# Rounds of five attention units with expert tiles in a new order, in a fused transformer block on one core

## The chip, the core and the metric

The kernel runs on one core of a Trainium2 chip. The metric is the device time of one execution in microseconds. TensorE is called PE, VectorE DVE, ScalarE ACT, GpSimd POOL, and SyncE, which here issues most DMA transfers, SP.

## The reference

The reference is a pre-norm transformer block over 2048 tokens of width 512, all in float32. After a layer norm, two parts run on the same normalised tokens, and both results are added to the input:

```python
xn = _layernorm(x)
x  = x + attention(xn) + moe(xn)

# attention: 16 heads, each with two score maps (q1,k1), (q2,k2) of width 16
s      = einsum('bthd,bshd->bhts', q, k) * scale          # q, k with interleaved rotary
a      = softmax(where(causal, s, NEG))
attn_i = concatenate([a_i @ v1, a_i @ v2])                # i = 1, 2; 32 columns per head
f      = rfft(attn1, axis=tokens) - lambda * rfft(attn2, axis=tokens)
attn   = irfft(f * gaussian_filter, axis=tokens)
attn   = attn * rsqrt(mean(attn*attn over a head's 32) + eps) * rms_weight * (1 - LAMBDA_INIT)
out    = attn @ Wout

# moe: 8 experts of inner width 352, top 2 of a softmax gate with renormalised weights
y      = sum_k topk_w[k] * (silu(x @ w1[e_k]) * (x @ w3[e_k])) @ w2[e_k]
shared = (silu(x @ sw1) * (x @ sw3)) @ sw2                # inner width 704
```

## The kernel before

**Stages.** The first 366 us hold the layer norm, the projections, the gate with its top-2, the rotary step and the first tokens of the shared expert. The stage that the change is mostly about is `middle(general=False)`: attention scores and values, with the experts' work laid between them. `ending()` then runs the token filter as products with fixed matrices (`product`, L1141), the head norm (`Pair`), the output projection (`projected`, L1270) and the last additions (`finished`, `last`).

**Who decides the order.** In `middle` and in `ending` the schedule is written by hand: PE, DVE, ACT, POOL (in `middle` SP too) execute their instructions in the order in which the Python code calls them, each waiting for what it needs. There is no reordering. Buffers come from pools that rotate: a new tile of a tag takes the oldest buffer and waits until its last reader is done.

**Attention units.** Work is cut by `turns`: eight groups `g` of two heads, and in each the query chunks `qc` = 3, 2, 1, 0 of 512 tokens. A turn consists of units (`Chunk.units`); a plain unit is one head and one block of 128 keys against 512 queries. Near the diagonal, units have fewer columns and are masked. There are 544 units (`stream`). For a unit, `scores` multiplies keys with queries for both score maps (PE, `ps_s`, L822), takes the exponential on ACT (L835, `pt`) and, where masked, zeroes what lies above the diagonal on POOL (`affine_select`, L840). `values` multiplies both heads' `pt` with the values (PE, `ps_o`, L862, 4 products for each block of keys, each of which is two instructions in the profile). `added` sums the exponentials over keys on DVE (L876, L879). When a turn ends, `sums` (PE, `ps_sum`, L888), `finish` (PE transposes into `ps_ot` and `ps_st`, then DVE: reciprocal `rcp` L903, `o_n` L908) and `put` (POOL, L917) follow. When a group's four turns have ended, `folded` does the group's butterflies over the tokens in steps on POOL, the last group's on DVE (L947 to L970).

**A round.** The loop at L1029 takes four units: `burst` of two (their scores), the `values` of the oldest turn that are due, a turn's `sums`, `burst` of the other two, the remaining `values`, then `put`, `finish`, the adds (those of masked units at the end), and steps of the experts' work (`work`), as many as keep pace with the share of `stream` that is done. Then come up to two steps of `folded`. At the first unit of a turn, `burst` also issues on SP the loads of the next turn's queries (`load_queries`: 8 transfers `qS` of 64 KB) and of the next group's keys (`load_keys`: 4 transfers `kS` of 128 KB, which read each row for two places of the tile by a leading broadcast of 2).

**Experts.** `experts()` is a generator that yields between pieces of work. It runs the shared expert for tokens 512 to 1919, then 34 tiles (`NR`) of 128 routed tokens. The first 28 (`NP`) hold tokens of one expert, the last 6 of two experts, 64 rows each. The rows are gathered by `rows_of` (POOL). A tile goes through a transpose (`ps_x`, L165), two up products (`xh` and `xg`, L180), an activation and a multiplication (`xtanh` on ACT and DVE), a transpose (`ps_u`, L206, copied as `uT` by DVE), the down product (`xy`, L216) and a store (`y_sb`, scaled on ACT, to `ys`). Weights lie in two buffers, `w_sb[0]` and `w_sb[1]`, each with an up part `wu` (1408 KB) and a down part `wd` (768 KB). Tiles of one expert take the buffers in turn; a tile of two experts uses both at once. `fetch_up` for the next but one half is issued on SP behind the `xg` products, and `fetch_down` behind `xy`. In the remaining 128 tokens, `kept`, the shared expert runs in `ending` (`several`, PE `wh` L246).

**PSUM.** There are 8 banks: scores have two buffers of two banks (`sps`), `ps_o` one, and everything else in `middle` shares the three banks of `fps` by `bank()`, in a fixed rotation: `wh`, `wy`, `ps_x`, `xh`, `xg`, `ps_u`, `xy`, `ps_sum`, `ps_ot`, `ps_st`.

**The end stage.** In `ending`, pools `t1`, `tp` serve all tiles in SBUF. `still(k)` issues the loads and gathers for later output tiles (`fetched`: query rows on SP, accumulating transfers on POOL). `across` transposes a scaled tile for `projected`; `Pair` starts with `y` and its square, and `means` and `scales` make the norm.

Of the kernel before, what the change touches and what calls it, by code (L numbers as in the profile page):

```python
# [19 lines left out]
P = 128  # L20
T = 2048
E = 512
# [24 lines left out]

NP = (T * TOP // HALF - NX) // 2
WUP = NE * 2 * FI
WCOL = WUP + NF * E  # L50
# [17 lines left out]
def block_kernel(  # L68
# [527 lines left out]
    def middle(general):  # L596


        with ExitStack() as pools:
# [29 lines left out]
            def experts():  # L629
# [7 lines left out]
                for t0 in range(EARLY, NT - 1, TQ):  # L637
                    t1 = min(t0 + TQ, NT - 1)
                    last = t1 == NT - 1
                    cols = slice(t0 * P, t1 * P)  # L640
                    for n, us in enumerate(chunks(xnT[:, :, cols], u_last)):
                        if last and n == 0:
                            who_sb = mp.tile([P, E], F32, tag="x", name="who_sb")
                            who_sb = who_sb[:NR].rearrange("n (k p o) -> n k p o", k=TOP, o=2)
                            for k in range(TOP):
                                nc.sync.dma_start(who_sb[:, k], who[k][: NR * P, :].rearrange("(n p) o -> n p o", p=P))
                        elif last and n == 2:
                            nc.vector.tensor_add(who_sb[:, 0], who_sb[:, 0], who_sb[:, 1])
                        elif last and n == 3:
                            ps = bank([P, 2, NR], "ps_w")  # L650
                            for i in range(2):
                                nc.tensor.transpose(ps[:, i, :], who_sb[:, 0, :, i], ident[:NR, :NR])
                            nc.vector.tensor_copy(tok, ps[:, 0, :])
                            nc.vector.tensor_copy(wcol, ps[:, 1, :])
                        elif last and n == 5:


                            xr = [rows_of(0), rows_of(1)]
                            es = [routed(0)]
                            fetch_up(es[0], 0, nc.sync)  # L660
                        yield 3.45 * (t1 - t0) / TQ
                    if last:
                        es.append(routed(2))
                        fetch_up(es[1], 1, nc.sync)
                    for t in range(t0, t1):
                        y = result(us, t - t0, range(NF))
                        yield 2.6
                        stored(result(us, t - t0, range(NF, SCH), y), ysh[t], 0.5)
                        yield 2.6
# [7 lines left out]

                sets = [[j] if j < NP else [2 * j - NP, 2 * j - NP + 1] for j in range(NR)]
                halves = [2 * j + i for j in range(NR) for i in range(len(sets[j]))]

# [3 lines left out]
                def tile_down(j, uT):  # L684
                    return places(j, 1), uT, ys[j * P : (j + 1) * P, :], wcol[:, j : j + 1]

                for j in range(NR):
# [5 lines left out]
                    if j + 2 < NR:  # L693
                        xr.append(rows_of(j + 2))
                    for n in sets[j]:
# [61 lines left out]
            def greatest(g, qc):  # L757
# [29 lines left out]
                return shift  # L787

            class Chunk:

# [19 lines left out]

                def scores(self, unit):
# [4 lines left out]
                    ps = sps.tile([P, 2, QC], F32, tag="sc", name="ps_s")  # L816
                    for h, kb, off, col, w in unit:
                        for s in range(2):
                            r = slice(64 * s, 64 * s + 64)
                            k = keys[2 * g + h, kb // TQ][r, kb % TQ * P : (kb % TQ + 1) * P]  # L820
                            to = ps[:, s, col : col + w]
                            nc.tensor.matmul(  # L822
# [11 lines left out]
                    used = slice(min(c for *_, c, _ in unit), max(c + w for *_, c, w in unit))  # L834
                    nc.scalar.activation(pt[:, :, used], ps[:, :, used], AF.Exp, scale=SCALE)  # L835
                    for _, kb, _, col, _ in unit:
                        if kb >= qc * TQ and not general:

                            part = pt[:, :, col : col + P]
                            nc.gpsimd.affine_select(  # L840
                                out=part, in_=part, pattern=[[0, 2], [1, P]], compare_op=ALU.is_ge, fill=0.0,
                                base=0, channel_multiplier=-1,
                            )
# [140 lines left out]
            for c in range(NQC):  # L984
                load_keys(0, c)
                if c == 0:
                    load_queries(0, NQC - 1)
            worked, begun, summed, held = 0.0, -1, 0, []
            todo, closing, closed, shared, ready, folding = [], [], [], [], [], None

            def burst(units):
                nonlocal begun
                found = []
                for n, chunk, unit in units:
                    if n > begun:
                        begun = n
                        if n + 1 < len(turns):
                            load_queries(*turns[n + 1])

                        if chunk.g + 1 < NG:  # L1000
                            load_keys(chunk.g + 1, (chunk.qc + 1) % NQC)
                    found += chunk.scores(unit)
                return found
# [12 lines left out]

            def masked(entry):
                _, c, unit = entry
                return any(kb >= c.qc * TQ for _, kb, *_ in unit)

            def added(entries):
# [6 lines left out]

            for i in range(0, len(stream), 4):  # L1029
                units = stream[i : i + 4]  # L1030
                found = burst(units[:2])
                n, ended = values()
# [3 lines left out]
                if n < 2 and not closing:  # L1036

                    work()
                found += burst(units[2:])
                while todo:  # L1040
# [10 lines left out]
                added(before)  # L1051
                added(u for u in units[:2] if not masked(u))
                later = [u for u in units[2:] if not masked(u)]
                while True:
                    work()
                    added(later[:1])
                    later = later[1:]
                    if worked / (work_all - left) >= (i + 4) / len(stream):
                        break
                added(later)  # L1060
                added(u for u in units if masked(u))
                if any(map(masked, units)) or not shared:
                    steps = 0
                else:
                    steps = 1 if any(map(masked, stream[i + 4 : i + 8])) else 2
                for _ in range(steps):
                    if folding is None and ready:
                        folding = folded(ready.pop(0), nc.gpsimd)
                    if folding is not None and next(folding, 0) == 0:
                        folding = None  # L1070
# [20 lines left out]
    def ending():  # L1091

        with tc.tile_pool(name="tail1", bufs=1) as t1, tc.tile_pool(name="tail", bufs=2) as tp, tc.tile_pool(
            name="tail_ps", bufs=4, space=PSUM
        ) as fps, tc.tile_pool(name="conv_ps", bufs=2, space=PSUM) as zps, tc.manual_schedule(
            engines={mybir.EngineType.PE, mybir.EngineType.DVE, mybir.EngineType.Activation, mybir.EngineType.Pool}
# [3 lines left out]
            nc.scalar.dma_start(conv[:, 11 * P :], conv_t[:, 11 * P :])  # L1102
            _, _, _, _, (_, _, stored), _ = expert(tp, fps)
            hidden, gated, times, _, result = shared_expert(tp, fps, 2)
            fetch_down(wex[NX + 1 : NX + 2], 1, nc.scalar)
# [46 lines left out]
            def copied(z):  # L1152
                diff = tp.tile([P, 2, E], F32, tag="diff", name="diff")
                nc.scalar.copy(diff, z)
# [27 lines left out]
            product(zr[:, 1, :], [(1, vd[:, 1, :])])  # L1182
            first = tp.tile([P, E], F32, tag="first", name="first", bufs=1)
            nc.scalar.copy(first, zr[:, 1, :])
# [127 lines left out]
            for n in range(NT // 2):  # L1312
# [157 lines left out]
```

## Time and profile before

| quantity | value |
|---|---|
| time, median of 3 runs | 1360.07 us (1357.98 to 1361.46) |
| profiled execution, own time | 1360.14 us |
| its span | 1358.3 us, 1.84 us less than its own time |
| granted TensorE clock, mean | 0.994 |
| PE busy in the span | 1312.6 us (97%) |
| DVE, ACT, POOL busy | 1005.4, 688.4, 626.3 us |
| 366 to 1186 us (units beside experts) | PE 808.43 of 820, DVE 667.37, ACT 534.43, POOL 492.18 |
| 1186 to 1242 us (last units and expert tiles) | PE 47.61 of 56 |
| 1242 to 1358 us (end stage) | PE 102.80 of 116, DVE 78.48, POOL 69.63 |

The durations are of one profiled execution, whose time lies 0.07 us from the median. In the profile's rows, "L822" is the line of the program that issued the instruction, `out<-in` names what it writes and reads, and a row that ends in "x4" joins four neighbouring instructions of one kind.

### The profile page before, as it was taken

The page shows a single profiled execution, that of the slowest core. Times are in us where ns is not written, and L with a number is a line of the kernel's source. Part 1 is how long each engine was busy: PE and PEld are TensorE (multiplying, and loading weights), DVE is VectorE, ACT ScalarE, POOL GpSimd, SP SyncE. Part 2 cuts the span into 40 slices and gives each one's busy share as a digit, 9 for nine tenths or more (in the row PEclk, how much of TensorE's full clock was granted, in tenths as well). Part 3 has the DMA queues.
Part 4 walks back from the last instruction along what each step waited for, and adds up shares of the span by engine and source line. Part 5 has one row for each costly group of instructions (what it writes and reads, how often), then busy time and mean ns, then how long its engine had stood idle before and what let it go on. Part 6 is the DMA issues. An engine that isn't in the chain of part 4 may idle for free.

```text
span 1358.3 us, 20810 instructions
## 1 busy us (share of the span) xinstructions
PE 1312.6 (97%) x7554; PEld 600.3 (44%) x7554; DVE 1005.4 (74%) x1344; ACT 688.4 (51%) x847; POOL 626.3 (46%) x671
## 2 busy tenths in 40 slices
PE   7999999999999999999999999899999999987998
PEld 3444444334443444445444444344544444443544
DVE  7049883287668778868889986778898788764785
ACT  2311110265656566676666666566676666640221
POOL 0002330012221323235968984778589469421764
PEclk9999999999999999999999999999999999998999
DMA  9406673200211122235665656555565666777997
GB/s 375 171 16 171 201 196 97 89 15 32 75 43 31 40 75 82 74 123 170 190 194 143 226 176 180 181 173 174 185 194 178 210 189 230 262 294 293 175 219 169
DMA packets 75578, 214.29 MB, mean 158 GB/s; under 512 B 12244, under 2 KB 12696, under 8 KB 69576
## 3 DMA queue, kind: packets, MB, share of 16 engines
q1 hardware_dynamic: 62744, 185.68, 41.7%
q0 software_dynamic: 11056, 22.78, 8.6%
q10 hardware_dynamic: 1664, 4.38, 0.9%
q8 instruction: 63, 1.03, 0.3%
q14 instruction: 51, 0.42, 0.1%
HBM read 169.69 MB, written 43.10 MB: 157 GB/s over the span
## 4 chain that ended last, share of the span: by engine, by line
PE 65%; DVE 6%; POOL 5%; DMA 3%; issue 1%; ACT 1%; SPq 0%; DVEq 0%; ACTq 0%; POOLq 0%
PE ps_o L862 16%; PE ps_s L822 12%; PE wh L246 8%; PE xy L216 6%; PE xg L180 5%; PE xh L180 5%; PE wy L284 4%; PE ps_sum L888 2%; DMA wu<-in_wex_dram 2%; POOL pt L840 1%; PE po L1270 1%; DMA wd<-in_wex_dram 1%; DVE sum L879 1%; PE ps_ot L900 1%; PE ps_x L165 1%
## 5 line engine op out<-in xcount | busy, mean ns | idle before, releaser
L879 DVE TENSOR_TENSOR sum<-sum,pt 128x1024 f32<-128x1024 f32 (+3 forms) x576 | 621.4, 1128 | 36.3 <-ACT pt L835 21.6
L835 ACT ACTIVATE pt<-ps_s 128x1024 f32<-128x1024 f32 x544 | 527.3, 1023 | 184.3 <-PE ps_s L822 131.0
L840 POOL TENSOR_SCALAR_AFFINE_SELECT pt<-pt 128x256 f32<-128x256 f32 x256 | 171.0, 693 | 358.7 <-ACT pt L835 357.5
L862 PE MATMUL ps_o<-pt,vd 128*32 128x512 f32 (+3 forms) x2560 | 268.0, 534 | 4.1 <-POOL pt L840 4.1
L822 PE MATMUL ps_s<-qS,kS 64*128 64x512 f32 (+3 forms) x1280 | 203.8, 406 | 2.0 <-DVEq L1335 1.6
L822 PEld LDWEIGHTS ps_s<-qS,kS 64*128 64x128 f32 x1280 | 97.1, 185 | 177.0 <-issue 95.9
L246 PE MATMUL wh<-xnT,wu 128*128 128x512 f32 (+1 forms) x352 | 150.4, 574 | 0.0
L862 PEld LDWEIGHTS ps_o<-pt,vd 128*32 128x32 f32 x2560 | 66.9, 109 | 125.8 <-issue 103.5
L545 PE MATMUL ps_x<-xnT,wqk_sb 128*128 128x512 f32 x256 | 110.5, 593 | 0.0
L498 POOL DMA_INDIRECT who<-pairs,slot x32 | 33.1, 1034 | 165.9 <-DVE pairs L495 104.9
L216 PE MATMUL xy<-wd,uT 128*128 128x512 f32 (+3 forms) x240 | 97.1, 606 | 7.7 <-DVE rcp L903 6.3
L246 PEld LDWEIGHTS wh<-xnT,wu 128*128 128x128 f32 x352 | 64.1, 190 | 72.7 <-issue 56.5
L180 PE MATMUL xh<-wu,xT 128*128 128x352 f32 (+1 forms) x320 | 90.5, 473 | 4.2 <-DMA wu<-in_wex_dram 3.3
L917 POOL TENSOR_TENSOR vd<-o_n 128x128 f32<-128x128 f32 x60 | 62.2, 1057 | 65.6 <-DVE o_n L908 65.5
L180 PE MATMUL xg<-wu,xT 128*128 128x352 f32 (+1 forms) x320 | 88.6, 468 | 0.0
L545 PEld LDWEIGHTS ps_x<-xnT,wqk_sb 128*128 128x128 f32 x256 | 48.4, 190 | 60.6 <-issue 60.6
L284 PE MATMUL wy<-wd,ws 128*128 128x512 f32 x160 | 74.8, 603 | 0.0
L257 DVE SCALAR_TENSOR_TENSOR ws<-ws,wh 128x512 f32<-128x512 f32 (+4 forms) x26 | 16.7, 644 | 73.6 <-ACT ws L256 73.6
L1125 POOL DMA_INDIRECT res<-ys,slot x32 | 54.9, 1715 | 25.3 <-DMA res<-ysh 13.5
L562 ACT CAST hi<-turned 128x1024 fp32r<-128x1024 f32 x16 | 16.7, 1045 | 93.9 <-DVE turned L560 70.9
L180 PEld LDWEIGHTS xh<-wu,xT 128*128 128x128 f32 (+1 forms) x320 | 48.0, 176 | 31.7 <-issue 6.5
L180 PEld LDWEIGHTS xg<-wu,xT 128*128 128x128 f32 (+1 forms) x320 | 46.6, 174 | 34.4 <-issue 14.8
(254 smaller groups left out, 1416.8 us busy)
## 6 DMA issues: line engine op xcount, KB each, us to landing
wu<-in_wex_dram SPq DMA_DIRECT2D x44, 1408.0 KB
wd<-in_wex_dram SPq DMA_DIRECT2D x43, 768.0 KB
kS<-parts_k SPq DMA_DIRECT2D x128, 128.0 KB
qS<-parts_q SPq DMA_DIRECT2D x256, 64.0 KB
ys<-y_sb SPq DMA_DIRECT2D x34, 256.0 KB
parts_q<-hi SPq DMA_DIRECT2D x32, 256.0 KB
parts_k<-hi SPq DMA_DIRECT2D x16, 256.0 KB
parts_k<-turned SPq DMA_DIRECT2D x16, 256.0 KB
```

Source lines behind the costliest of these rows:

```text
L180: nc.tensor.matmul(dst[r, :], xT[:, c, r], w[:, o : o + FI], start=(c == 0), stop=(c == NE - 1), skip_group_check=True,)
L216: nc.tensor.matmul(y[r, :], uT[:m, ic, r], w[:m, ic * E : (ic + 1) * E], start=(ic == 0), stop=(ic == NF - 1), skip_group_check=True,)
L246: nc.tensor.matmul(dst, w_sb[o // WUP][0][:, o % WUP : o % WUP + P], x[:, c, :], start=(c == 0), stop=(c == NE - 1))
L284: nc.tensor.matmul(y, us[i][:, t * P : (t + 1) * P], w_sb[i // NF][1][:, i % NF * E : (i % NF + 1) * E], start=(i == 0), stop=(i == SCH - 1),)
L545: nc.tensor.matmul(ps[:, i, :], wqk_sb[st, qk][:, i, c, :], xnT[:, c, cols], start=(c == 0), stop=(c == NE - 1),)
L822: nc.tensor.matmul(to, k, queries[2 * g + h, qc][r, off : off + w], start=True, stop=not general)
L835: nc.scalar.activation(pt[:, :, used], ps[:, :, used], AF.Exp, scale=SCALE)
L840: nc.gpsimd.affine_select(out=part, in_=part, pattern=[[0, 2], [1, P]], compare_op=ALU.is_ge, fill=0.0, base=0, channel_multiplier=-1,)
L862: nc.tensor.matmul(self.o[r : r + 32, off:], vd[:, kb, v0 : v0 + 32], pt[:, s, :], start=first, stop=self.ended, skip_group_check=True,)
L879: nc.vector.tensor_add(to, to, pt)
L917: eng.tensor_add(vd[:, self.qc * TQ : (self.qc + 1) * TQ, v0 : v0 + 32], self.o_n[:, :, h, 0, :], self.o_n[:, :, h, 1, :],)
L1125: nc.gpsimd.indirect_dma_start(out=came[k], out_offset=None, in_=ys, in_offset=bass.IndirectOffsetOnAxis(ap=slot[:, step - 2, order[k] : o ...
```

## The change

The change has five parts.

- **Order of the tiles.** `ORDER` puts the six tiles of two experts first, then the 28 of one expert. The rows gathered, the weights loaded, the places in `ys` and the routing weights follow it.
- **Rounds.** A round takes five units, three in the first burst and two in the second (`many`, `ahead`). The third unit of the first burst (`apart`) writes its scores into two banks of `fps` (named `ps_a`), and its exponential is two instructions of 128x512 instead of one of 128x1024.
- **Selects.** For the masked unit whose two parts lie at columns 0 and 256, one `affine_select` over 128x4x128 elements takes the place of two.
- **Adds and folding.** The adds of the first burst's units, masked ones among them, come right away; only masked units of the second burst are added last. The number of `folded` steps is counted by whether the round and the following one are free of masked units.
- **End stage.** `ws`, `diff` and `first` have a pool of their own (`tail2`), the last `y_sb` is scaled by ACT instead of DVE, `finished(2n-1)` and `still(2n-1)` come before `across` and `prepared`, and `means()` comes after `finished(2n)` and `still(2n)`.

```diff
+ORDER = [*range(NP, NR), *range(NP)]
...
-                            xr = [rows_of(0), rows_of(1)]
-                            es = [routed(0)]
+                            xr = [rows_of(j) for j in ORDER[:2]]
+                            es = [routed(2 * ORDER[0])]
                             fetch_up(es[0], 0, nc.sync)
...
-                        es.append(routed(2))
+                        es.append(routed(2 * ORDER[0] + 1))
                         fetch_up(es[1], 1, nc.sync)
...
-                sets = [[j] if j < NP else [2 * j - NP, 2 * j - NP + 1] for j in range(NR)]
-                halves = [2 * j + i for j in range(NR) for i in range(len(sets[j]))]
+                sets, halves = [], []
+                for tj in ORDER:
+                    n = 1 if tj < NP else 2
+                    sets.append(range(len(halves), len(halves) + n))
+                    halves += [2 * tj + i for i in range(n)]
...
+                    if apart:
+                        banks = [bank([P, QC], "ps_a") for _ in range(2)]
+                    else:
+                        ps = sps.tile([P, 2, QC], F32, tag="sc", name="ps_s")
+                        banks = [ps[:, s] for s in range(2)]
...
+                    if apart:
+                        for s in range(2):
+                            nc.scalar.activation(pt[:, s, used], banks[s][:, used], AF.Exp, scale=SCALE)
+                    else:
+                        nc.scalar.activation(pt[:, :, used], ps[:, :, used], AF.Exp, scale=SCALE)
+                    if masked(self, unit) and not general:
+
+                        cols = [col for *_, col, _ in unit]
+                        if cols == [0, 2 * P]:
+                            chosen = [pt.rearrange("p s (h q) -> p (s h) q", h=2)[:, :, :P]]
+                        else:
+                            chosen = [pt[:, :, col : col + P] for col in cols]
...
+            many = 4 if general else 5
+            ahead = many - 2
...
-                for n, chunk, unit in units:
+                for k, (n, chunk, unit) in enumerate(units):
...
-                    found += chunk.scores(unit)
+                    found += chunk.scores(unit, k == 2)
...
-            for i in range(0, len(stream), 4):
-                units = stream[i : i + 4]
-                found = burst(units[:2])
+            for i in range(0, len(stream), many):
+                units = stream[i : i + many]
+                found = burst(units[:ahead])
...
-                added(u for u in units[:2] if not masked(u))
-                later = [u for u in units[2:] if not masked(u)]
+                added(units[:ahead])
+                later = [u for u in units[ahead:] if not masked(*u[1:])]
...
-                added(u for u in units if masked(u))
-                if any(map(masked, units)) or not shared:
-                    steps = 0
-                else:
-                    steps = 1 if any(map(masked, stream[i + 4 : i + 8])) else 2
-                for _ in range(steps):
+                added(u for u in units[ahead:] if masked(*u[1:]))
+                following = stream[i + many : i + 2 * many]
+                steps = [shared and not any(masked(*u[1:]) for u in some) for some in (units, following)]
+                for _ in range(sum(map(bool, steps))):
...
-            _, _, _, _, (_, _, stored), _ = expert(tp, fps)
-            hidden, gated, times, _, result = shared_expert(tp, fps, 2)
+            _, _, _, _, (_, _, stored), _ = expert(tp, fps, by_scalar=True)
+            hidden, gated, times, _, result = shared_expert(t2, fps, 2)
...
+                if ahead is not None:
+                    finished(2 * n - 1, ahead)
+                    still(2 * n - 1)
                 if n + 1 < NT // 2:
                     aT = across(2 * n + 2)
                 if n + 2 < NT // 2:
                     pairs.append(prepared(n + 2))
-                if ahead is not None:
-                    finished(2 * n - 1, ahead)
-                    still(2 * n - 1)
-                if n + 2 < NT // 2:
-                    pairs[n + 2].means()
                 if n + 1 < NT // 2:
                     now, po = po, projected(after)
                     finished(2 * n, now)
                     still(2 * n)
+                if n + 2 < NT // 2:
+                    pairs[n + 2].means()
```

More of the change, by code (lines that the diff above doesn't have):

```diff
@@ L684, in tile_down @@
                 def tile_down(j, uT):
-                    return places(j, 1), uT, ys[j * P : (j + 1) * P, :], wcol[:, j : j + 1]
+                    tj = ORDER[j]
+                    return places(j, 1), uT, ys[tj * P : (tj + 1) * P, :], wcol[:, tj : tj + 1]
                 for j in range(NR):
@@ L693, in experts @@
                     if j + 2 < NR:
-                        xr.append(rows_of(j + 2))
+                        xr.append(rows_of(ORDER[j + 2]))
                     for n in sets[j]:
@@ L787, in greatest, with masked @@
                 return shift
+            def masked(chunk, unit):
+                return any(kb >= chunk.qc * TQ for _, kb, *_ in unit)
             class Chunk:
@@ L809, in units, with scores @@
                             yield [(h, kb, 0, 0, QC)]
-                def scores(self, unit):
+                def scores(self, unit, apart):
                     g, qc = self.g, self.qc
@@ L815, in scores @@
                         self.shift = greatest(g, qc)
-                    ps = sps.tile([P, 2, QC], F32, tag="sc", name="ps_s")
+                    if apart:
[3 more added lines that the diff above has]
+                        banks = [ps[:, s] for s in range(2)]
                     for h, kb, off, col, w in unit:
@@ L820, in scores @@
                             k = keys[2 * g + h, kb // TQ][r, kb % TQ * P : (kb % TQ + 1) * P]
-                            to = ps[:, s, col : col + w]
+                            to = banks[s][:, col : col + w]
                             nc.tensor.matmul(
@@ L834, in scores @@
                     used = slice(min(c for *_, c, _ in unit), max(c + w for *_, c, w in unit))
[L835 to L839, printed above, removed]
+                    if apart:
[9 more added lines that the diff above has]
+                            chosen = [pt[:, :, col : col + P] for col in cols]
+                        for part in chosen:
                             nc.gpsimd.affine_select(
-                                out=part, in_=part, pattern=[[0, 2], [1, P]], compare_op=ALU.is_ge, fill=0.0,
-                                base=0, channel_multiplier=-1,
+                                out=part, in_=part, pattern=[[0, part.shape[1]], [1, P]], compare_op=ALU.is_ge,
+                                fill=0.0, base=0, channel_multiplier=-1,
                             )
@@ L1015, in work @@
                 worked += next(ex, work_all)
-            def masked(entry):
-                _, c, unit = entry
-                return any(kb >= c.qc * TQ for _, kb, *_ in unit)
             def added(entries):
@@ L1038, in middle @@
                     work()
-                found += burst(units[2:])
+                found += burst(units[ahead:])
                 while todo:
@@ L1057, in middle @@
                     later = later[1:]
-                    if worked / (work_all - left) >= (i + 4) / len(stream):
+                    if worked / (work_all - left) >= (i + many) / len(stream):
                         break
                 added(later)
-                added(u for u in units if masked(u))
-                if any(map(masked, units)) or not shared:
-                    steps = 0
-                else:
-                    steps = 1 if any(map(masked, stream[i + 4 : i + 8])) else 2
-                for _ in range(steps):
+                added(u for u in units[ahead:] if masked(*u[1:]))
+                following = stream[i + many : i + 2 * many]
+                steps = [shared and not any(masked(*u[1:]) for u in some) for some in (units, following)]
+                for _ in range(sum(map(bool, steps))):
                     if folding is None and ready:
@@ L1091, in ending @@
     def ending():
-        with tc.tile_pool(name="tail1", bufs=1) as t1, tc.tile_pool(name="tail", bufs=2) as tp, tc.tile_pool(
-            name="tail_ps", bufs=4, space=PSUM
-        ) as fps, tc.tile_pool(name="conv_ps", bufs=2, space=PSUM) as zps, tc.manual_schedule(
+        with tc.tile_pool(name="tail1", bufs=1) as t1, tc.tile_pool(name="tail2", bufs=2) as t2, tc.tile_pool(
+            name="tail", bufs=2
+        ) as tp, tc.tile_pool(name="tail_ps", bufs=4, space=PSUM) as fps, tc.tile_pool(
+            name="conv_ps", bufs=2, space=PSUM
+        ) as zps, tc.manual_schedule(
             engines={mybir.EngineType.PE, mybir.EngineType.DVE, mybir.EngineType.Activation, mybir.EngineType.Pool}
@@ L1152, in copied @@
             def copied(z):
-                diff = tp.tile([P, 2, E], F32, tag="diff", name="diff")
+                diff = t2.tile([P, 2, E], F32, tag="diff", name="diff")
                 nc.scalar.copy(diff, z)
@@ L1182, in ending @@
             product(zr[:, 1, :], [(1, vd[:, 1, :])])
-            first = tp.tile([P, E], F32, tag="first", name="first", bufs=1)
+            first = t2.tile([P, E], F32, tag="first", name="first", bufs=1)
             nc.scalar.copy(first, zr[:, 1, :])
```

## The prediction

> **What bounds the kernel.** I read the page's engine table and chain shares first, then TensorE's order of work in one round, the waits that end on PE, the transfers on the chain behind 1170 us, and last a stretch in which a turn's key loads run.
>
> ```profile
> PE 1312.6 (97%) x7554; PEld 600.3 (44%) x7554; DVE 1005.4 (74%) x1344; ACT 688.4 (51%) x847; POOL 626.3 (46%) x671
> PE 65%; DVE 6%; POOL 5%; DMA 3%; issue 1%; ACT 1%; SPq 0%; DVEq 0%; ACTq 0%; POOLq 0%
> ```
>
> PE is busy for 97% of the span; from 366 to 1186 us for 808.4 of 820, at a granted clock of 1.00. So a term counts if it removes time in which PE runs, or makes PE wait. Other engines count only where PE waits for them (VectorE is busy for 667 of those 820, ScalarE 534, GpSimd 492).
>
> PE's timeline in a round, by start and duration:
>
> ```profile
> 803.78 0.73 PE L822 MATMUL ps_s<-qS,kS 64*128 64x512 f32 x4
> 804.44 1.92 PE L862 MATMUL ps_o<-pt,vd 128*32 128x512 f32 x16
> 806.29 0.73 PE L822 MATMUL ps_s<-qS,kS 64*128 64x512 f32 x4
> 806.96 2.63 PE L180 MATMUL xg<-wu,xT 128*128 128x352 f32 x8
> ```
>
> Start to start, two units of scores take 0.66 us, 16 value matmuls 1.85 to 1.86; groups of 8 take 1.00 elsewhere. Two eights cost 2.00 and one sixteen 1.85, so a block of values has a fixed cost of 0.15. Score blocks show theirs less well: 0.33 per unit, but blocks of four, six or eight matmuls all lie between 0.66 and 0.72.
>
> The last tiles of the experts, each with two experts' weights, make PE wait:
>
> ```profile
> 1173.66 8.46 DMA wd<-in_wex_dram
> 1184.46 10.78 DMA wu<-in_wex_dram
> 1195.28 4.27 PE xh L180 x14
> 1206.44 10.38 DMA wu<-in_wex_dram
> 1216.87 2.60 PE xh L180 x14
> 1229.57 8.55 DMA wd<-in_wex_dram
> 1238.16 2.81 PE xy L216 x10
> 1241.76 5.25 DMA ys<-y_sb
> ```
>
> A tile with two experts occupies both weight buffers; the next up-weights (two of 1408 KB) go out only when xg is through, and land 10.4 to 10.8 us later. The xh block begun at 1191.81 took 7.67 us, where one with its weights there takes 2.52: 5.2 lost. At 1215.38 it lost 1.5. From the last ps_st (1224.58) to ps_r (1241.78) are 17.2 us with 11.8 of work: 5.4. Together 12.
>
> **What the change makes of it.** *Rounds of five.* PE's instructions as built have 218 score blocks instead of 272 and 128 value blocks instead of 152; the products stay. The values give 24 x 0.15 = 3.6. With a third unit at 0.33 the score blocks give nothing; at 0.21, as the block of eight hints (0.72 for 2.2 times a four's instructions), 109 x 0.12 = 13. I take 0.24: 10. Sum **-14**, between 0 and -17. The third unit's exp is split: 2 x 0.591 (the 128x512 copy on ScalarE) for 1.023, 0.16 x 109 = 17 us of ScalarE, hidden by its idle time (286 of 820); if not hidden it would delay the release of banks, which is counted there. The rule that a change of tiling mode drains TensorE (Trainium skill, "TensorEngine Tiling (Array Packing)", Key Properties) speaks for a gain from every avoided block. It has no price; if each of the 54 + 24 avoided blocks drained for the 0.15 that the value rows show, the estimate by it would be 11.7, which lies inside the range and is not used.
>
> *Merged selects, earlier masked adds.* 32 of 256 selects go from GpSimd (0.693 us each), which is 46% busy; PE's waits for a select sum to 4.1 us in four places. An add ahead of the others can hold VectorE's queue until the select is through; behind it stand xtanh, rcp and uT, for which PE waits. PE's waits for rcp are 6.3 us in all:
>
> ```profile
> PE xy L216 <- DVE rcp L903: 6.3, 4, 3.3
> PE ps_o L862 <- POOL pt L840: 4.1, 4, 1.6
> PE xh L180 <- DMA wu<-in_wex_dram: 3.3, 2, 2.7
> ```
>
> From -4 to +6; I take 0, since shifts in both directions stand there.
>
> *The tail.* The last tiles are then of one expert, double buffered: most of the 12 goes. What is next late is the folding of the last group on VectorE, which ran from 1228.66 to 1237.28 and must be over before ps_r; PE's new order lays products with the kept tokens beside it. **-11** (-8 to -13).
>
> *The end stage.* Its PE gaps are 2.55 (1249.75, where ws waits for the buffer that the ys store holds), 0.93, 1.88, 0.24, 1.27 and 0.50. The separate pool takes away the first; y_sb on ScalarE takes 0.68 off VectorE, which the chain passes through (ms, a, y at about 1.2 each). `finished` now stands ahead of `prepared`, releasing a po bank about one 1.2 us operation earlier; behind it the `out` stores on SP and the loads and gathers of `still` (SP, GpSimd) go out as much earlier. These queues work in order and nothing is moved behind them (GpSimd is busy for 69.6 of the stage's 116 us), so I cost that at nothing; if GpSimd were full, it would be the same late gather as now. `means` is later by an add, which may cost 0.5 to 1 per pair if the chain goes that way. **-5** (0 to -7).
>
> *Two-expert tiles at the start.* Here the tail's waits return with less between. PE's new order puts, between the end of xg(j) and xh(j+1), for j = 0 to 5: 0.9, 7.1, 7.4, 13.0, 11.7 and 12.4 us of work by the block times above. The load of two halves needs 10.4 to 10.8 by the chain; the engines' full rate in a stretch where both streamed (425 GB/s at 1165 to 1200 us) makes it 6.8, so no case is below 0.9 + about 6 of waiting at the second tile. Against it speaks also what is queued on SP: the keys and queries of the next turns stand ahead of the weights in the new SP order. How a key load behaves, in the window 658 to 680 us of before (DMA busy tenths in 40 slices, then SP's issues):
>
> ```profile
> DMA  5631111149932999999996999994111101111379
> 658.46 2.37 SPq L727 DMA_DIRECT2D kS<-parts_k  x4
> 662.18 0.36 SPq L146 DMA_DIRECT2D wu<-in_wex_dram  x1
> 668.16 0.34 SPq L149 DMA_DIRECT2D wd<-in_wex_dram  x1
> ```
>
> The four kS transfers (512 KB, 256 rows of 2 KB each out of a leading broadcast of two) leave a mean busy share near 0.1, that is 2 engines of 16, for 11 to 13 us; the wu issued at 662.18 landed at about 677.9, 15.7 later, where one half unhindered takes about 5. So a weight load begun beside them waits on those two engines. The rule behind the row is in the Trainium skill, "DMA: Bandwidth & Descriptors", Rules for kernel authors: an outermost dimension of c below 16 confines a transfer to c engines; by it these loads keep to two engines in the new place too, and a transfer laid out over 128 partitions would not; without that confinement the wait below would be 9.6 in place of 17, and the sum 8 lower. SP also stood 12.21 us in issuing the eight qS at 610.09, which holds a weight load behind it.
>
> Second tile: 18 needed (about 15.7 plus the half's remaining 2 to 3) minus 0.9 = **17** (9.6 by 10.5 alone; 25 if SP is held as well). Third and fourth together: 3 each by 10.4 minus 7.1 or 7.4 = **6** (0 at 6.8; 8). Fifth: a turn's key loads again, 20 minus 13 = **7** (0 to 10). Sixth 0; to the first single tile **2** (0 to 6), as its down weights share the queue. Lead **+32** (+13 to +42, the ends not all at once). Whatever of it goes is lost whole: PE has no other order to follow. What it covers on VectorE (the backlog of adds) is not on the path.
>
> *Banks.* Two more tenants a round, 534 instead of 316 over the middle stage for three banks in a fixed ring. By the order, the time between PE's last write to a bank and its next use falls from 8 to 10 us (median) to about 3.4. The consumers' release times in before, after PE's write: uT copies 1.8 (median; a quarter over 3.8), xg's multiply 1.1 (a tenth over 3.6), ps_ot 1.6, ps_x 1.6, y_sb 0.73. Most fit into 3.4. About 110 tenants whose consumer is a VectorE operation behind adds (1.128 us each) meet it late; with a quarter of those late by 0.5 and the remainder of late ScalarE releases, I take **+14**; -4 if the new order happens to relieve rcp, +28 if every fourth of the 218 waits 0.5 us.
>
> Sum: -14 + 0 - 11 - 5 + 32 + 14 = **+16**. Profiled execution: 1360.14 for a span of 1358.3, which is on the median 1360.07. Predicted span about 1374, time **1376**. Something of 4 us (0.3%) is what a measurement of this kernel can tell from no change.
>
> **Rivals.**
> A, faster: the lead costs no more than the tail did. For it: the weights' 10.4 includes sharing with other loads; the floor is 6.8, and SP may issue the keys so early, at a turn's start, that they are through. Then lead 10, banks 4: -14 - 11 - 5 + 10 + 4 = -16, **1344**. It decides if the second tile waits below 10 us and the other five hardly. Against: 15.7 us in the window above.
> B, nothing: lead 24, banks 6: 0, **1360**.
> C, slower by more: the ring of banks decides. A score block that needs two banks at once stands in PE's order ahead of values and experts; if half of the 109 rounds wait 0.7 us (+38) and the third unit costs 0.33 (rounds -4), lead 32, tail -11, end -5: +50, **1410**. Against: PE's idle time from 366 to 1186 us is 11.6 in all, with the ring as it is.
>
> **How the numbers follow.** Forecast 0.50 (1362 to 1390), A 0.27, B 0.10, C 0.13. Faster by over 0.3%: A and a little of the forecast's low side, 0.28; same: B, 0.10; slower 0.62. The range reaches to 3 us below A's middle, 1341, and to C's near side, 1402; out of it are about 0.3 of A (0.08), 0.7 of C (0.09) and a hundredth of the forecast: 0.18.
>
> **What would show it.** Right: in the trace after, xh of the second expert tile waiting for DMA wu 15 us or so near 607 us, its chain with wu rows there and none at 1184 or 1206; the two-row gap before ps_r below 2; 218 score blocks, a block of three units near 0.9 us start to start; PE waits for ACT or DVE on banks, ps_s <- ACT pt or xh <- DVE uT, of some 14 us altogether. Wrong: xh waits under 10 us in the lead stage altogether (A); blocks of three at 1.0 (no gain of rounds); waits for banks over 25 (C); or VectorE becoming what PE waits for throughout.

## The result, and the profile after

The changed kernel takes 1439.22 us (median of 4 runs, 1434.18 to 1443.71) against 1360.76 before: ratio 1.058, interval 1.053 to 1.063. It is slower, as forecast, but by 79 us instead of 16, outside the range. The profiled execution took 1434.18 with a span of 1432.4, 74.1 above before's.

The page after, engine table and chain shares:

```profile
PE 1323.9 (92%) x7554; PEld 615.7 (43%) x7554; DVE 1012.7 (71%) x1343; ACT 691.9 (48%) x957; POOL 586.8 (41%) x639
PE 60%; DMA 9%; DVE 7%; issue 3%; ACT 2%; POOL 1%; SPq 0%; ACTq 0%; DVEq 0%; POOLq 0%
```

PE is still the bound, but idle for 8% instead of 3%, and busy 11 us longer with the same 7554 instructions. The waits of PE in after (in total, times, longest):

```profile
PE xh L182 <- DMA wu<-in_wex_dram: 32.0, 6, 14.7
PE ps_a L836 <- DVE uT L211: 19.4, 8, 5.4
PE ps_a L836 <- issue: 5.1, 2, 3.7
PE ps_a L836 <- ACT pt L851: 4.2, 2, 2.1
PE ps_u L208 <- DVE xtanh L199: 2.7, 1, 2.7
PE xy L218 <- DMA wd<-in_wex_dram: 2.6, 1, 2.6
```

Two kinds are new: up-weights in the lead (the six two-expert tiles that now come first, and the first single one behind them), and the third unit's score banks, `ps_a`. The windows of 600 to 760 us, before and then after, show why PE is busy longer:

```profile
600.00:760.00 160.00, 157.21 (x1137) 76.57 (x1134) 140.47 (x165) 106.72 (x130) 121.98 (x131) 1.00 0.59 178
```

```profile
600.00:760.00 160.00, 121.01 (x901) 51.74 (x894) 96.75 (x115) 74.49 (x104) 60.65 (x73) 0.87 0.62 209
```

The column behind POOL is the granted clock: 1.00, then 0.87. In the clock's records it is halved for 3.4 us or a multiple of that, nearly always behind a wait of PE. I add up PE's pauses over 0.1 us up to its last product, and for the half clock half of the time in which PE worked under it, which is an estimate:

| | before | after | difference |
|---|---|---|---|
| pauses of PE | 40.2 us | 102.9 us | +62.7 |
| lost to the half clock (13.7 and 88.7 us long) | 6.6 | 31.6 | +25.0 |
| everything else (by subtraction from the span) | | | -13.6 |
| span | 1358.3 | 1432.4 | +74.1 |

### The profile page after: what moved, and what is told of

Same layout as the page of the kernel before. It is cut to its first block, busy times and chain, and to the rows that moved or that the text cites. A ratio compares the mean times of both kernels' runs of the same rounds, so it can differ in the third digit from the quotient of the medians.

```text
span 1432.4 us, 20896 instructions
## 1 busy us (share of the span) xinstructions
PE 1323.9 (92%) x7554; PEld 615.7 (43%) x7554; DVE 1012.7 (71%) x1343; ACT 691.9 (48%) x957; POOL 586.8 (41%) x639
## 4 chain that ended last, share of the span: by engine, by line
PE 60%; DMA 9%; DVE 7%; issue 3%; ACT 2%; POOL 1%; SPq 0%; ACTq 0%; DVEq 0%; POOLq 0%
PE ps_o L884 16%; PE ps_s L836 8%; PE wh L248 7%; PE xg L182 6%; PE xy L218 6%; PE xh L182 5%; DMA wu<-in_wex_dram 4%; PE wy L286 4%; DVE sum L901 3%; PE po L1291 2%; PE ps_a L836 2%; DMA wd<-in_wex_dram 2%; PE ps_sum L910 2%; ACT pt L853 1%; PE ps_ot L922 1%
## 5 line engine op out<-in xcount | busy, mean ns | idle before, releaser
L901 DVE TENSOR_TENSOR sum<-sum,pt 128x1024 f32<-128x1024 f32 (+2 forms) x576 | 627.9, 1139 | 23.9 <-POOL pt L862 11.1
L853 ACT ACTIVATE pt<-ps_s 128x1024 f32<-128x1024 f32 x435 | 423.8, 1028 | 167.6 <-PE ps_s L836 124.8
L862 POOL TENSOR_SCALAR_AFFINE_SELECT pt<-pt 128x256 f32<-128x256 f32 (+1 forms) x224 | 183.0, 841 | 506.2 <-ACT pt L853 441.2
L836 PE MATMUL ps_s<-qS,kS 64*128 64x512 f32 (+3 forms) x1022 | 163.8, 406 | 5.5 <-DMA qS<-parts_q 3.8
L836 PEld LDWEIGHTS ps_s<-qS,kS 64*128 64x128 f32 x1022 | 77.4, 185 | 149.8 <-issue 91.9
L182 PE MATMUL xh<-wu,xT 128*128 128x352 f32 (+1 forms) x320 | 99.5, 515 | 36.8 <-DMA wu<-in_wex_dram 32.0
L851 ACT ACTIVATE pt<-ps_a 128x512 f32<-128x512 f32 x218 | 119.8, 611 | 23.8 <-PE ps_o L884 13.6
L925 DVE RECIPROCAL rcp<-ps_st 128x16 f32<-128x16 f32 x32 | 8.3, 259 | 112.9 <-PE ps_st L923 112.9
L836 PE MATMUL ps_a<-qS,kS 64*128 64x512 f32 (+3 forms) x258 | 53.1, 376 | 31.2 <-DVE uT L211 19.4
L192 ACT ACTIVATE xtanh<-xh 128x352 f32<-128x352 f32 x34 | 15.8, 465 | 102.9 <-PE xh L182 90.6
```

Source lines behind the costliest of these rows:

```text
L182: nc.tensor.matmul(dst[r, :], xT[:, c, r], w[:, o : o + FI], start=(c == 0), stop=(c == NE - 1), skip_group_check=True,)
L836: nc.tensor.matmul(to, k, queries[2 * g + h, qc][r, off : off + w], start=True, stop=not general)
L851: nc.scalar.activation(pt[:, s, used], banks[s][:, used], AF.Exp, scale=SCALE)
L862: nc.gpsimd.affine_select(out=part, in_=part, pattern=[[0, part.shape[1]], [1, P]], compare_op=ALU.is_ge, fill=0.0, base=0, channel_multip ...
L901: nc.vector.tensor_add(to, to, pt)
```

## The experiments

Ratios are to the kernel before, run on the same chip; 0.01 is 13.6 us.

**Which part costs what.** Four kernels undo a part or do it alone.

```diff
# e1: after, old order            # e2: after, rounds of four
-ORDER = [*range(NP, NR), *range(NP)]
+ORDER = [*range(NR)]
-            many = 4 if general else 5
+            many = 4
# e3: before, with all that ORDER needs;  e4: before, with the new ending()
```

> The changed kernel with the tiles in the old order, two-expert tiles last. Theory S (stalls and the clock they cost): the lead stage's waits for wu and wd (38 us of PE idle time in the trace after, and 11 us for the half clock granted behind them) go, the tail's 8 us of idle time and its 3 us of half clock come back: 1439 - 49 + 11 = about 1401. Theory P (the prediction's prices: lead 32, tail 11, nothing for the clock): 1418. Theory B (the ring of banks makes nearly all of the loss, the tiles' order little): over 1425.

> The changed kernel with rounds of four units, no scores in the experts' banks; the new order of tiles, adds and end stage stay. Theory S: the waits on banks (about 40 us of idle time outside the lead stage, 14 us of half clock) go, the 13 us that the rounds of five save in block costs are lost: 1439 - 54 + 13 = about 1398. Theory P (banks 14, rounds -14): 1439. Theory B: 1360 to 1380.

> The kernel before with the new order of the tiles alone. Theory S: lead stage +38 of idle time and +11 of half clock, tail -11: 1360 + 38 = about 1398. Theory P: +21, 1381. Theory B: within 10 us of before.

> The kernel before with the new end stage alone. All theories: -5 or -6 us, 1354 to 1356, since the end stage is 5.9 us shorter from trace to trace; if the end stage's gain came only from what the rest had finished earlier, 1360.

| run | median us | ratio (interval) |
|---|---|---|
| e1, after with the old order | 1416.37 | 1.0414 (1.039 to 1.0439) |
| e2, after with rounds of four | 1392.19 | 1.0232 (1.0211 to 1.0254) |
| e3, the order alone | 1389.39 | 1.0222 (1.0193 to 1.0251) |
| e4, the end stage alone | 1357.61 | 0.9984 (0.997 to 0.9997) |

The order alone costs 30 us, 9 more than the prediction's +32 - 11; taken out of the changed kernel (e1) it gives back 23. Rounds of five cost 47 (1.058 less 1.0232), where the prediction's -14 + 14 came to nothing. Theory B falls, since e2 and e3 are far above before; theory S had the order too dear by 9 (e3) to 15 us (e1) and the rounds too cheap by 6 (e2). The end stage alone gains 2.2 us, not 5.

**Who holds the banks.** In after, VectorE and then PE around 1213 us:

```profile
1195.47 17.43 DVE L901 TENSOR_TENSOR sum<-sum,pt 128x1024 f32<-128x1024 f32 x13
1212.83 0.41 DVE L210 COPY uT<-ps_u 128x256 f32<-128x256 f32 x1
1213.16 0.27 DVE L211 COPY uT<-ps_u 96x128 f32<-96x128 f32 x1
```

```profile
1202.23 0.55 PE L208 MATMUL ps_u<-cst,xtanh 128*128 128x128 f32 x3
1207.44 0.73 PE L836 MATMUL ps_s<-qS,kS 64*128 64x512 f32 x4
1213.58 1.13 PE L836 MATMUL ps_a<-qS,kS 64*128 64x512 f32 x2 [5.41 <-DVE uT L211]
```

ps_u is written by 1202.8; its copy stands behind 13 adds without a pause and is done 10.7 us after that. The ring comes back to that bank at about 1208, for ps_a, and PE stands for 5.41. In before, 7 of 34 such copies end more than 4 us after ps_u, the latest 7.4, and no row of PE's waits names uT; in after 15 of 34 end so late. e5 takes the copies out of VectorE's queue; e6 puts the masked adds last again.

```diff
# e5, on after
-            nc.vector.tensor_copy(uT[:, :2, :], ps[:, :2, :])
-            nc.vector.tensor_copy(uT[:96, 2, :], ps[:96, 2, :])
+            nc.scalar.copy(uT[:, :2, :], ps[:, :2, :])
+            nc.scalar.copy(uT[:96, 2, :], ps[:96, 2, :])
# e6, on after
-                added(units[:ahead])
+                added(u for u in units[:ahead] if not masked(*u[1:]))
...
-                added(u for u in units[ahead:] if masked(*u[1:]))
+                added(u for u in units if masked(*u[1:]))
```

> The changed kernel with the two copies out of ps_u (uT) on ScalarE instead of VectorE. Theory Q (PE stands at ps_a because the bank of ps_u is freed by a VectorE copy that is queued behind a run of adds): the 19 us of waits of ps_a for uT and the 5 us put down to issue go, and with each of these about ten waits 1.7 us of half clock: 1439 - 24 - 15 = about 1400. Rival (the ring is simply too short, whoever empties it; the next tenant is late instead): within 8 us of 1439. Rival (ScalarE's exponentials now delay xh and the scores): above 1439.

> The changed kernel with the adds of masked units last again, as in the kernel before. If the early masked adds, which can hold VectorE's queue until GpSimd's select is through, make the waits on banks: 10 to 20 us faster, 1420 to 1429. If only the ring's shortness and the adds' number before uT count: within 6 us of 1439; the run with rounds of four (1392) against the new order of tiles alone (1389) with an end stage worth 2 to 5 speaks for about 5.

e5: 1410.27, ratio 1.0379 (1.0345 to 1.0413): 27 us less from two small copies moved. None of the 34 copies is over 4 us late now. So what stands ahead of the copy on VectorE makes them late, not the ring's length alone. Other late releases remain:

```profile
PE ps_a L836 <- DVE xtanh L193: 6.9, 2, 5.9
PE ps_x L167 <- DVE xtanh L199: 3.7, 2, 2.4
```

e6: 1459.71, ratio 1.0737 (1.0719 to 1.0755): 20 us slower, against both expectations. The early masked adds are worth 20 us within rounds of five. By the trace that is 17 us of pauses and 7 of half clock. The added pauses are spread:

```profile
PE xh L182 <- DMA wu<-in_wex_dram: 36.0, 6, 16.0
PE ps_a L836 <- DVE uT L211: 22.4, 10, 4.5
PE ps_a L836 <- issue: 8.2, 2, 6.9
PE xy L218 <- DVE rcp L925: 3.7, 3, 1.9
```

Against after these are 4.0, 3.0, 3.1 and 3.7 us more. 13 copies of uT are late instead of 15, so uT alone isn't the cause; why the order of the adds moves all of them is not shown. In rounds of four they are worth nothing that shows (e2 against e3 with e4: 1.0232, and 1.0222 - 0.0016).

**Why the lead waits.** Chain of waits in e3, 600 to 760 us, its transfers:

```profile
610.01 16.70 DMA wu<-in_wex_dram
678.89 18.89 DMA wu<-in_wex_dram
731.28 16.77 DMA wu<-in_wex_dram
```

These three tiles (second, fifth, seventh; my expectation of e7 miscounts two of them) are those whose loads meet a turn's keys. e7 and e8 issue each key load as two transfers without the broadcast.

```diff
# e7, on e3
-                        nc.sync.dma_start(
-                            k[64 * s : 64 * s + 64, :].bitcast(F32),
-                            src.unsqueeze(0).to_broadcast([2, 2 * D, QC]),
-                        )
+                        for rep in range(2):
+                            r = 64 * s + 32 * rep
+                            nc.sync.dma_start(k[r : r + 32, :].bitcast(F32), src)
# e8: the same, the new ending(), and
+ORDER = [*range(8), *(j for i in range(6) for j in (NP + i, 8 + i)), *range(14, NP)]
# e11: before with the split keys alone;  e14: after with the split keys
```

> The kernel before with the new order of tiles, and each key load issued as two transfers of 32 partitions instead of one with a leading broadcast of two. Theory K (key loads on two of sixteen engines hold the weight loads that are queued behind them): the waits of the second, fourth and sixth tile's xh (10.8, 14.3 and 11.9 us in the run with the order alone) fall to about 8, 2 and 2, and the half clock behind the last two goes: 1389 - 25 - 5 = about 1360. Rival (SP's own issuing of 8 queries and now 8 keys holds the weights): 1385 to 1400.

> The kernel before with the new end stage, key loads in two transfers, and the two-expert tiles each between two tiles of one expert, from the ninth tile on. Theory S with K: neither lead nor tail waits for weights: 1360 - 11 (tail) - 3 (end stage) = about 1346. Rival (a two-expert tile waits about 4 us wherever it stands, as one of its halves is loaded late): 1346 + 6 x (4 + 1.7) = 1380. Prediction's price of the tail without clock: 1349.

> The kernel before with the key loads issued as two transfers of 32 partitions each and nothing else. Theory K: single tiles have a tile's time for their weights, so little goes; the tail's loads have no keys beside them: 1358 to 1361. Rival (more issues on SP delay the weights): 1363 or more.

> The changed kernel with key loads in two transfers. Theory K: as with the order alone (1389 to 1365), the lead loses about 24 us of 35 us of waits and their half clock, the waits on banks stay: 1439 - 24 - 8 = about 1407. Rival (in the changed kernel the weights wait for SP's issues or for both buffers anyway): within 10 us of 1439.

| run | median us | ratio (interval) |
|---|---|---|
| e7, order and split keys | 1364.64 | 1.0043 (1.0023 to 1.0064) |
| e14, after and split keys | 1407.57 | 1.0345 (1.0328 to 1.0362) |
| e11, before and split keys | 1358.69 | 0.9999 (0.9985 to 1.0013) |
| e8, split keys, pairs between singles, new end | 1354.72 | 0.9958 (0.9944 to 0.9973) |

Chain of e7 over the same stretch:

```profile
609.20 9.48 DMA wu<-in_wex_dram
...
673.14 8.65 DMA wu<-in_wex_dram
...
715.02 6.71 DMA wu<-in_wex_dram
```

PE's waits for up-weights, e3 and then e7:

```profile
PE xh L182 <- DMA wu<-in_wex_dram: 37.0, 5, 12.4
```

```profile
PE xh L182 <- DMA wu<-in_wex_dram: 11.4, 5, 3.1
```

From 16.7 to 18.9 down to 6.7 to 9.5: the same bytes in the same order on SP, with twice the issues for keys. That settles theory K: 24 us in e7, 32 in e14, and nothing in e11, where weight loads meet keys too but single tiles have a tile's time for them: there, as in before, PE waits for weights only in the tail. e8 left two waits for wu, 9.2 us together, where theory S expected none.

**The half clock.** e10 and e13 put products of a constant tile into xh's bank ahead of the true ones, so that PE works while it waits. They add only that work.

```diff
# on e3, in up_half
+            for _ in range(fill):
+                nc.tensor.matmul(
+                    dst, ident, kept.rearrange("p c t -> p (c t)")[:, :FI], start=True, stop=True, skip_group_check=True
+                )
# fill by tile number: e10 {1: 12, 3: 19, 5: 18}, e13 {1: 17, 4: 22, 6: 18}
```

> The kernel before with the new order of tiles alone, and in the banks of the second, fourth and sixth tile's xh 12, 19 and 18 extra products of a constant tile before the true ones, so that PE works (about 7.4, 11.7 and 11 us) where it would wait 7.8, 12.4 and 11.9 for weights. Theory C (half the clock is granted for some us after a wait of over about 2 us of PE): the half-clock rows behind these waits go and with them the 8 us they cost: 1389 - 8 = about 1381, although PE does more. Rival (the records of the clock cost nothing, or the waits alone count): 1389 to 1392.

> The kernel before with the new order of tiles alone, and 17, 22 and 18 products of a constant tile in the bank of xh of the second, fifth and seventh tile ahead of the true ones: 10.4, 13.5 and 11.1 us of work where PE waited 10.8, 14.3 and 11.9 us. Theory C (half clock behind a wait costs time): the half-clock rows there go, and the 8 us that they cost: 1389 - 8 = about 1381, with 35 us more of PE work. Rival (the records of the clock cost nothing): 1389 to 1392.

e10: 1409.4, 1.0358 (1.0328 to 1.0388). Two of its three fillers stand at tiles that had not waited, so it is 20 us of plain extra work and tells nothing. e13: 1389.71, 1.0218 (1.0195 to 1.0241), like e3: 8 us of gain were expected and none came. The rows of the second tile, e3 and then e13:

```profile
622.31 1.41 PE L182 MATMUL xh<-wu,xT 128*64 128x352 f32 x2 [7.80 <-DMA wu<-in_wex_dram]
626.75 4.40 PE L182 MATMUL xh<-wu,xT 128*64 128x352 f32 x14 [3.04 <-DMA wu<-in_wex_dram]
```

```profile
614.60 10.33 PE L180 MATMUL xh<-kept,cst 128*128 128x352 f32 x34 [0.44 <-DVE o_n L918]
624.85 0.81 PE L186 MATMUL xh<-wu,xT 128*64 128x352 f32 x2
627.18 2.58 PE L186 MATMUL xh<-wu,xT 128*64 128x352 f32 x14 [1.52 <-DMA wu<-in_wex_dram]
```

The same 14 products take 4.40 us behind the wait and 2.58 where PE had been kept at work. At the end of the three tiles e13 is 3.0 us ahead of e3; the eighth tile's xy starts at 801.8 instead of 807.4, as a wait of 2.09 us with a half clock behind it, at 785 us in e3, is gone too. Later 3.4 of these 5.6 us go again, as two waits (3.27 us for rcp, 1.88 in the end stage) are followed by a half clock, as 3.27 and 1.78 us at the same places of e3 were not. Over the whole trace the constant products take 34.3 us, PE's pauses are 31.1 us shorter and the half clock's loss is 6.3 us smaller (11.4 to 5.1). So the filling was 3 us longer than what it filled and ate half of the gain; the two spans, 1387.3 and 1385.5, differ by 1.8. The slowness behind a wait is shown in the rows; its worth in the whole time is not.

**Put together.** e9 is after with e5's copies, split keys and e8's order. e12 is e8 with `means()` back in its old place and

```diff
+ORDER = [*range(4), *(j for i in range(6) for j in (NP + i, *range(4 + 4 * i, 8 + 4 * i)))]
```

> The changed kernel with uT copied by ScalarE, key loads in two transfers, and the two-expert tiles each between two of one expert. If lead, uT and half clock are what the change lost, and the rounds' saving of 8 to 13 us is real: from 1410 (uT on ScalarE) the 34 us of waits for wu and about 12 of half clock go: about 1364. If the rounds of five were worth having once their waits are cut, it would be under the 1355 of the interleaved kernel with rounds of four; I expect it is not, as xtanh, ws and the sums still free banks late.

> The kernel before with the key loads in two transfers, the new end stage but means() where it was, and each two-expert tile followed by four of one expert (from the fifth tile on). Theory S: the two waits of 4.6 us that were left with the alternating order go as the queue has more time, with 3 us of half clock, and the end stage's wait of 2.8 us at across: 1355 - 9 - 3 - 4 = about 1340; if a two-expert tile waits where it meets a turn's queries and keys, whatever follows it: 1350 to 1355.

e9: 1362.37, 1.0025 (1.0012 to 1.0038), as expected: with its three costs repaired, the change is about even. e8, with rounds of four and the old adds and copies, stays better by 8 to 9 us. e12: 1353.76, 0.9959 (0.994 to 0.9978), against 1340 expected. Waits for wu fell from 9.2 to 4.1 us, the one for `a` at across only from 4.6 to 3.3. e8 and e12 are faster than before by 0.4%. How much of that is the place of the two-expert tiles is barely clear of noise: with split keys and the tiles at the end it is 0.9999 (e11), and the new end stage alone brings 0.0016.

## Why the prediction was wrong

**Rounds, -14: right.** In after, three units take 0.89 us start to start (0.895 as the median of 64 blocks of full units) and two 0.66, so the third costs 0.23 (0.24 taken); 24 value matmuls take 2.71, 0.14 less than an eight and a sixteen. A round in after:

```profile
894.60 0.73 PE L836 MATMUL ps_s<-qS,kS 64*128 64x512 f32 x4
895.17 0.39 PE L836 MATMUL ps_a<-qS,kS 64*128 64x384 f32 x4
895.49 2.78 PE L884 MATMUL ps_o<-pt,vd 128*32 128x512 f32 x24
898.20 0.79 PE L836 MATMUL ps_s<-qS,kS 64*128 64x384 f32 x8
```

The -13.6 left over in the sum agrees.

**Banks, +14: the term that failed.** Waits of ps_a alone are 31.2 us in after, and the half clock behind them comes on top, so that five units in a round cost 47 us net. From e2's trace, with rounds of four, to after's, PE's pauses grow by 35.0 us and the half clock's loss by 16.0: 51 us, where the term had 14. The step took the median release and put "a quarter of those late by 0.5", about 27 waits of 0.5 us; there were 14 waits of ps_a, of 2.2 us on average. For adds come in runs, 13 of them in 17.43 us in the stretch above, and a copy behind a run waits for all that is left of it. e5 shows it: 27 us hung on uT. Rival C named the ring with +38 for waits, without uT or the clock.

**Half clock: a missing term, +25 by the records.** "Whatever of it goes is lost whole" counted a wait as its length. Before's trace had the sign: 13.7 us at half clock, four times, each behind a wait of 2.3 to 3.3 us. So had the prediction's own tail: it took whole block times, and 5.2 us lost at one xh held a wait of only 2.67. The Trainium skill, "TensorE: Matmul & The Clock Gate", What's actually happening, has free-running windows of 3413 ns, which is the length seen here; its advice (Why this matters for your kernels) to allow no gaps over about 3 us is too mild for these runs, where waits of 2.0 us in after, and two under 1.8, were followed by 3.4 us or more at half clock. e13 leaves open how much of the 25 would come back if waits alone were filled. Of these 25 us, 16 are the ones counted under the banks.

**Lead, +32: right in size.** xh waited 16.6 us at the second tile (17 taken), 2.0 at the third and 0 at the fourth (6), 7.0 at the fifth (7), 0 at the sixth, 6.4 at the first single one (2, the one that was too small). The reason given, keys on two engines, is what e7 shows. The prediction put 8 us on it, at the second tile alone (17 less 9.6 is 7.4); splitting the loads in after brought 32 (e14), with the waits for wu down from 32.0 to 8.3 us. That the forecast had the direction right rests on this term. The order alone cost 30 net instead of 21: in e3 the lead waits 37.0 us, and the half clock takes 4.8 us more than in before.

**Tail, -11: right** as far as the traces show: no weight load is on the chain behind 1250 us in after, and e3 has no pause of PE over 0.3 us from 1180 to 1276 us, where before lost 8 us and half clock on top. **End stage, -5: too much**; alone it brought 2.2 (0.4 to 4.1). In e4's trace the pauses of 2.55 and 1.88 us are gone, but the longest one at across is 2.83 us, with 1.27 before; that this makes the difference is not shown. **Adds, 0: wrong** in rounds of five, where they save 20 us (e6); in rounds of four nothing shows.

## What to carry to other kernels

Here a ring of buffers was as late as the longest runs of work queued ahead of its consumers, not as the median consumer: look for the longest run on the releasing engine before giving a ring more tenants, and move short releasing copies to another queue. The key loads with a leading broadcast kept about two of the sixteen DMA engines busy (a mean busy share near 0.1), and weight loads queued behind them took 16.7 to 18.9 us instead of 6.7 to 9.5; splitting them cost nothing here (e11). Tiles that need both weight buffers cost most at the start, where the loads of a turn's keys met them with little work to cover the wait; between tiles that need one they cost least here, by a margin barely clear of noise.

## What was not expected of the hardware

A pause of PE of 2 us or more was mostly followed by 3.4 us, or a multiple of that, at half the granted clock (4 of 4 such pauses in before, 16 of 17 in after, without the wait at the very start): 88.7 us of half clock in after, 13.7 in before. It was not always so: of two waits of 3.27 us for rcp, at 851 us in before and at 899 in e3, only the first was followed by one.
